# A graph layer on one core: 336 instead of 294 edge tiles picked on TensorE, their keys spread by DMA

## The chip, the cores and the metric

One core of one Trainium2 chip runs the whole kernel. The metric is device time in microseconds (us), median of the runs shown. Below, TensorE is PE in the profile, VectorE DVE, ScalarE ACT, GpSimd POOL and SyncE SP; PEld is TensorE's weight load.

## The reference

200,000 edges, sorted by destination, carry messages between 6,250 nodes of 64 features. Cut to what matters:

```python
w = silu(edge_attr_32 @ W1 + b1) @ W2 + b2                 # E x 9
h_src = x[src]                                             # a row of x for each edge
msg = einsum('ef,em,fmg->eg', h_src, edge_attr_9 * w, W_tp)
agg = segment_sum(msg, dst, 6250) / 4
emb = silu(node_vec[:, None] @ Wn1 + bn1) @ Wn2 + bn2      # gamma, beta
gamma, beta = split(emb, 2)
out = layernorm(x + agg * (1 + gamma) + beta)
```

## The kernel before

The edges form 1,563 tiles of 128, one edge to a partition, and 98 groups of 16 tiles (the last has 11). One stage `i` of the main loop works on several groups at once, as the program order has it: it gathers for group i+6, prepares i+2 and i+1, reduces i, and places i-2.

**Where `x[src]` comes from.** There are three ways, and a group uses all of them. For most tiles GpSimd issues one indirect DMA per tile (L91, `hs`), 13 a group. Every sixth group from 7 on (`SPG`, 16 groups) has its first tile loaded by SyncE row by row (L106), 128 DMAs of 256 bytes, spread over the six stages ahead with the register loads of L101. The last Q = 3 tiles of a group are *picked* by TensorE: x lies in SBUF in two fp32r parts `xs`, node number = 49 p + 7 h + l with p the partition. A tile's keys (p for each edge, and h times 128) are turned into a one-hot matrix, and 7 x 2 products of 448 columns (L482) with it fetch seven candidate rows for each edge into the PSUM tile `px`; VectorE selects the right one (L491, L493). So a picked tile costs 14 products, and an unpicked one an indirect DMA.

**How keys become one-hot matrices.** `setup` works out the keys on VectorE, turns them over on TensorE and writes them to DRAM (`kd`, L222 to L229) as bf16, the two halves in two rows. `load_keys` (L391) fetches two groups' keys onto two partitions. `keys` (L451) multiplies them with `ones2` (1 in two rows, 0 elsewhere; L458), so that every partition of the PSUM tile `pk` holds the sum of the halves for 384 edges; the fourth quarter of `pk` takes the product of `gate` (L357), and `gam` and `xb` are made from it (L358, L359). One VectorE instruction then compares the three tiles' keys with the seven node numbers of each partition (L464, `hot_k`).

**The order of the work.** The order is written by hand (`manual_schedule`), and each engine runs its instructions in that order. In stage i TensorE runs: the 14 products of pick 0 of group i+1, with `place(i-2)` (L559, `pd`) and `keys(i+2)` put between them; `hidden(i+2)` (L405); `second(i+1)` (L422); `windows(i)` (L511, `pz`), which needs all rows of group i; pick 1, with `weights(i+1)` (L432) and `project(i-1)` (L537, `pr`) between; pick 2. VectorE follows: `near` in even stages (L385), the addition of `pd` to `acc` (L563), `gam`, `xb`, `hot_k`, then L491 and L493 of pick 0, `weights` (L438, L444), `c` (L544), L491 and L493 of pick 1, in every fourth stage the ten operations of `finish_nodes`, then pick 2. ScalarE has `st` (L413), `p2s` (L425), eight copies `zt` (L521) and `r` (L542).

**Buffers.** PSUM has eight banks in use: `px` two, `pz` two, `p1` two, one under the tag "s" (`p2` of `second` and `weights`, and `pd`) and one under "r" (`pk` and `pr`). Who writes into "s" or "r" waits until the last reader of the tile before is done. `hs` has seven buffers, so GpSimd can be six groups ahead.

Of the kernel before, what the change touches and what calls it, by code (L numbers as in the profile page):

```python
# [6 lines left out]

F32 = mybir.dt.float32
I32 = mybir.dt.int32
BF16 = mybir.dt.bfloat16  # L10
F32R = mybir.dt.float32r
AF = mybir.ActivationFunctionType
ALU = mybir.AluOpType
AX = mybir.AxisListType

P = 128
N, F, M, D, H, E = 6250, 64, 9, 32, 64, 200000
NJ = 49
# [3 lines left out]
NBLK = (NT + KB - 1) // KB  # L22
# [3 lines left out]
FB = 2  # L26
AHEAD = 6
LB = 2
Q = 3
J = 7  # L30
SPG = range(7, NBLK, 6)
SPR = 22
# [16 lines left out]

def picked(g):  # L50

    return Q


def tiles(g):
# [4 lines left out]
def gnn_resnorm_kernel(ctx: ExitStack, tc: tile.TileContext, x, src, dst, dst_row, ea, sh, cn,  # L60
# [18 lines left out]
    with ExitStack() as fast:  # L79
# [35 lines left out]
        lo = keep.tile([P, NBLK], F32)  # L115
        nk = keep.tile([P, J], F32)
        li = keep.tile([P, J], F32)
        ones2 = keep.tile([P, P], BF16)
        kr2 = [keep.tile([P, LB, Q, P], BF16, name=f"kr{k}") for k in range(2)]
        zt = [keep.tile([P, 5, KB, W], F32, name=f"zt{k}") for k in range(2)]  # L120
        rel = keep.tile([P, NBLK * KB], F32)
        nid = keep.tile([P, NBLK], F32)
# [2 lines left out]
        ext = keep.tile([P, 4], F32)  # L125
        C = NBLK * Q
        jl = keep.tile([P, C], F32)
        kd = dram.tile([2, C, P], BF16, name="kd")
        cn_d = dram.tile([P, NJ], F32, name="cn_d")
        cn_v = cn_d.rearrange("p j -> (p j)")  # L130
        wn1c = keep.tile([H, 1], F32)
# [4 lines left out]
        def setup(temp):  # L136
# [52 lines left out]
            zero = temp.tile([P, 1], F32)  # L189
            nc.vector.memset(zero, 0.0)  # L190
            for k in range(2):
                nc.vector.memset(kr2[k], 0.0)
            nc.vector.memset(ones2, 0.0)
            nc.vector.memset(ones2[0:2], 1.0)
            for k in range(2):
                nc.vector.memset(zt[k][F:P, 4], 0.0)
                nc.vector.memset(ht[k][H:H + 1], 1.0)
            nc.vector.memset(wtc2[F:P, 4], 0.0)
# [20 lines left out]
            nc.vector.tensor_scalar(ti[1], rest, 37.0, None, op0=ALU.mult)  # L219
            nc.vector.tensor_scalar(ti[1], ti[1], 8, None, op0=ALU.logical_shift_right)  # L220
            nc.vector.tensor_scalar(kh, ti[1], float(P), None, op0=ALU.mult)
            for c0 in range(0, C, P):  # L222
                n = min(P, C - c0)
                p_kt = psum.tile([P, 2, P], F32, tag=("s", "r", "s")[c0 // P], name=f"p_kt{c0}")
                for i, half in enumerate((kp, kh)):
                    nc.tensor.matmul(p_kt[0:n, i, :], half[:, c0:c0 + n], ident, start=True, stop=True)
                kt = temp.tile([P, 2, P], BF16, name=f"kt{c0}")
                nc.scalar.copy(kt[0:n], p_kt[0:n])
                nc.sync.dma_start(kd[:, c0:c0 + n, :].rearrange("i c e -> c i e"), kt[0:n])  # L229
            nc.vector.scalar_tensor_tensor(jl, kh, -float(J) / P, rest, op0=ALU.mult, op1=ALU.add)  # L230
            hidden(0, act=False)
            load_keys(0)
# [33 lines left out]
            def between(h):  # L266

                if h == 0:
                    p_f = psum.tile([KB, NBLK], F32, tag="s", name="p_f")
                    nc.tensor.matmul(p_f, first_t, ident[0:NBLK, 0:NBLK], start=True, stop=True)  # L270
                    nc.scalar.copy(first_f, p_f)
                elif h == 1:
                    for f in keys(0, -1):
                        f()
                elif h == 3:
                    p_cn = psum.tile([P, NJ], F32, tag="s", name="p_cn")
                    nc.tensor.matmul(p_cn, cn_j, ident[0:NJ, 0:NJ], start=True, stop=True)
                    cn_s = temp.tile([P, NJ], F32)
                    nc.scalar.copy(cn_s, p_cn)
                    nc.sync.dma_start(cn_d, cn_s)  # L280
                    nc.sync.dma_start(wn1c, wn1.rearrange("o h -> h o"))
                    nc.sync.dma_start(bn1c, bn1.unsqueeze(1))
                    gate_load(0)
                    nc.sync.dma_start(wn2a[0:H, :], wn2)
                    nc.sync.dma_start(wn2a[H:H + 1, :], bn2.unsqueeze(0))
                    for q in range(2):
                        n = (M + 1 - q) // 2
                        nc.sync.dma_start(wtc2[q * F:(q + 1) * F, 0:n, :], wtp[:, q:M:2, :])
                    load(LB)
                    with nc.allow_non_contiguous_dma(reason="2048 words, once"):  # L290
                        nc.sync.dma_start(src_r, src[:, SPG[0] * KB:NBLK * KB:6 * KB].rearrange("p g -> g p"))
# [9 lines left out]
                    hidden_act(0)  # L301
                between(h)
            pick(0, 0)
            for f in keys(1, -1):
                f()
            base(0)
            near(0)
            second(0)
# [8 lines left out]
            ids()  # L317
            hidden(1)
            nc.scalar.copy(acc_r, zero.to_broadcast([P, NJ * F]))
            pick(0, 2)  # L320
            nc.sync.dma_start(xb, x.rearrange("(j p) f -> p j f", p=P))
            for s in range(2):
                nc.sync.dma_start(w2bd[s * H:(s + 1) * H, s, :], w2)
# [30 lines left out]
            nc.scalar.activation(ht[j0 // 4 % 2][0:H, :nj], cb.pop(j0)[:, :nj], AF.Silu, bias=bn1c, scale=wn1c)  # L354

        def gate(j, pe):
            nc.tensor.matmul(pe, ht[j // 4 % 2][:, j % 4], wn2a, start=True, stop=True)  # L357
            nc.vector.tensor_scalar(gam[:, j, :], pe[:, 0:F], 1.0, 0.25, op0=ALU.add, op1=ALU.mult)  # L358
            nc.vector.tensor_add(xb[:, j, :], xb[:, j, :], pe[:, F:2 * F])  # L359

# [29 lines left out]

        def load_keys(g):  # L391
            n = min(LB, NBLK - g)
            kr = kr2[g // LB % 2]
            nc.sync.dma_start(kr[0:2, 0:n].rearrange("i g t e -> i (g t) e"), kd[:, g * Q:(g + n) * Q, :])
            for i in range(n):
                kr_t[g + i] = kr[:, i, Q - picked(g + i):, :]

# [50 lines left out]

        hot_k = {}

        def keys(g, j):  # L451

            pk = psum.tile([P, Q + 1, P], F32, tag="r", name=f"pk{g}")
            q = picked(g)

            def part(k):
                if k == 0:
                    nc.tensor.matmul(pk[:, 0:q, :].rearrange("p t e -> p (t e)"), ones2,  # L458
                                     kr_t.pop(g).rearrange("i t e -> i (t e)"), start=True, stop=True)
                else:  # L460
                    gate(j, pk[:, Q, :])
                if k == n - 1:
                    hot_k[g] = late.tile([P, Q, J, P], F32R, tag="hot_k", name=f"hot_k{g}")
                    nc.vector.tensor_tensor(hot_k[g][:, 0:q], pk[:, 0:q].unsqueeze(2).to_broadcast([P, q, J, P]),  # L464
                                            nk[:, None, :, None].to_broadcast([P, q, J, P]), op=ALU.is_equal)

            n = 2 if 0 <= j < NJ else 1
            return [lambda k=k: part(k) for k in range(n)]

        def pick(g, t, other=()):  # L470


            other = [f for fs in other for f in fs]
            q = picked(g) if g < NBLK else 0
            if t >= q:
                for f in other:
                    f()
                return
            px = psum.tile([P, F, J], F32, tag="px", name=f"px{g}_{t}", bufs=2)
            for h in range(J):  # L480
                for i in range(2):
                    nc.tensor.matmul(px.rearrange("p f l -> p (f l)"), hot_k[g][:, t, h, :],  # L482
                                     xs[i][:, h].rearrange("p f l -> p (f l)"),
                                     start=(h == 0 and i == 0), stop=(h == J - 1 and i == 1))
                    if i == 1 and other:
                        other.pop(0)()
            for f in other:
                f()
            xm = late.tile([P, F, J], F32, tag="xm", name=f"xm{g}_{t}")
            c = (g + 1) * Q - q + t  # L490
            nc.vector.scalar_tensor_tensor(xm, li[:, None, :].to_broadcast([P, F, J]), jl[:, c:c + 1], px,  # L491
                                           op0=ALU.is_equal, op1=ALU.mult)
            nc.vector.tensor_reduce(hs[g][:, tiles(g) - q + t, :], xm, AX.X, ALU.add)  # L493
# [54 lines left out]
        def place(g):  # L548

            if not 0 <= g < NBLK:  # L550
                return []
            kb = lo_block(g)
            js = [j for j in (0, 1) if 0 <= kb + j < NJ]
            pd = {}

            def part(j):
                if j == js[0]:
                    pd[g] = psum.tile([P, 2, F], F32, tag="s", name=f"pd{g}")
                nc.tensor.matmul(pd[g][:, j, :], hot[g][:, j * P:(j + 1) * P], r[g], start=True, stop=True)  # L559
                if j == js[-1]:  # L560
                    hot.pop(g), r.pop(g)
                    b0, b1_ = kb + js[0], kb + js[-1] + 1
                    nc.vector.tensor_add(acc[:, b0:b1_, :], acc[:, b0:b1_, :], pd[g][:, js[0]:js[-1] + 1, :])  # L563

            return [lambda j=j: part(j) for j in js]

        done = 0
        with tc.manual_schedule(), tc.tile_pool(name="temp", bufs=1) as temp:
            setup(temp)

            for i in range(NBLK):
# [10 lines left out]
                for g in SPG:  # L582
                    if 0 < g - i <= AHEAD:
                        load_rows(g, (AHEAD - g + i) * SPR)
                pick(i + 1, 0, [place(i - 2)] + ([keys(i + 2, i - 2)] if i + 2 < NBLK else []))
                if 3 <= i <= 5:
                    reach(i - 3)
                if i + 2 < NBLK:
# [13 lines left out]
                while ready - done >= (FB if ready < NJ - 1 else 1):  # L602
                    finish(done, min(done + FB, ready))
                    done = min(done + FB, ready)
                pick(i + 1, 2)
                if i >= NBLK - 2:
                    windows(i)
                if i == NBLK - 2:
# [205 lines left out]
```

## Time and profile before

| | |
|---|---|
| median of 3 runs | 1590.99 us (1590.33 to 1592.33) |
| profiled execution, whole | 1590.71 us |
| its span, on which the profile's shares stand | 1588.9 us |
| TensorE clock granted, mean | 0.961 of full |
| SyncE row DMAs of 256 bytes (L106) | 2048 |
| `ea` loads (L374) | 49, of 512 KB |
| `kr` loads (L394) | 49, of 3 KB |
| DMA | 85.42 MB, mean 54 GB/s |

A group in the profile is all instructions of a line and an engine: count, busy time, mean duration in ns, then how long the engine had been idle before them and what ended that. Matmuls overlap, so that one instruction's duration is more than it adds to TensorE's time; the pitch between starts in the timeline is what counts. An fp32 matmul stands in the trace as two instructions.

### The profile page before, as it was taken

To read this page: it belongs to the slowest core of one execution; us is meant where nothing else is said; L and a number is where in the kernel's file an instruction comes from. 1 tells how busy PE (TensorE), PEld (TensorE's weight loads), DVE (VectorE), ACT (ScalarE), POOL (GpSimd) and SP (SyncE) were. 2 spreads that over 40 slices of the span, in tenths; PEclk is the share of its full clock that TensorE was granted. 3 is DMA by queue.
4 is the path that set the end of the run, shared out by engine and by line. 5 is a ranking of instruction groups with operands and counts; after the bars stand their busy time and mean duration, and the time that the engine had idled before them with its cause. 6 is when DMAs were issued, how large, how long until landed. Compare 5 with 4: busy or idle time off the path is not lost.

```text
span 1588.9 us, 33055 instructions
## 1 busy us (share of the span) xinstructions
PE 1407.5 (89%) x10206; PEld 1143.1 (72%) x10206; DVE 992.6 (62%) x1611; ACT 473.1 (30%) x1187; POOL 1186.0 (75%) x1262
## 2 busy tenths in 40 slices
PE   5999999988989888989898989888889899888886
PEld 3777778767777777777676767676777777776765
DVE  6676667665656565665665656656566666565664
ACT  4323223323232323232322323323223232322232
POOL 7777777777777777777777777777777777777773
PEclk9999999999999999999999999999999999999998
DMA  5312222221211121212111221121111211211110
GB/s 155 84 48 50 62 50 54 58 50 50 61 50 50 45 66 45 50 50 61 48 47 45 52 57 47 47 62 46 45 47 47 62 46 47 62 47 45 47 46 20
DMA packets 86199, 85.42 MB, mean 54 GB/s; under 512 B 37625, under 2 KB 52013, under 8 KB 86014
## 3 DMA queue, kind: packets, MB, share of 16 engines
q0 software_dynamic: 40096, 41.14, 11.7%
q1 hardware_dynamic: 45156, 40.44, 8.4%
q8 instruction: 83, 1.36, 0.4%
q10 hardware_dynamic: 762, 1.64, 0.3%
q14 instruction: 102, 0.84, 0.2%
HBM read 81.35 MB, written 1.78 MB: 52 GB/s over the span
## 4 chain that ended last, share of the span: by engine, by line
PE 33%; POOL 32%; issue 14%; DMA 10%; SPq 7%; DVE 2%; ACT 1%; POOLq 0%; ACTq 0%; DVEq 0%
POOL hs L91 32%; PE px L482 21%; DMA hs<-in_x_dram,src_i 9%; SPq L106 4%; PE pz L511 4%; PE pr L537 2%; PE p L405 2%; SPq L101 2%; PE p L422 1%; PE p L432 1%; PE pd L559 1%; DMA ea<-in_ea_dram 1%; DVE xm L491 0%; DVE hs L493 0%; PE pk L458 0%
## 5 line engine op out<-in xcount | busy, mean ns | idle before, releaser
L91 POOL DMA_INDIRECT hs<-in_x_dram,src_i x1253 | 1184.7, 945 | 382.6 <-issue 347.3
L482 PE MATMUL px<-xs,hot_k 128*128 128x448 f32 x4116 | 1100.4, 400 | 3.2 <-DVE xs L299 3.2
L482 PEld LDWEIGHTS px<-xs,hot_k 128*128 128x128 f32 x4116 | 717.9, 196 | 62.1 <-DVE xs L299 3.6
L491 DVE SCALAR_TENSOR_TENSOR xm<-li,jl,px 128x448 f32<-128x448 f32 x294 | 199.1, 677 | 213.0 <-PE px L482 211.2
L464 DVE TENSOR_TENSOR hot_k<-pk,nk 128x2688 fp32r<-128x2688 f32 x98 | 289.4, 2953 | 4.6 <-PE pk L458 4.6
L413 ACT ACTIVATE st<-p,b1c 128x1024 f32<-128x1024 f32 x98 | 109.1, 1114 | 560.1 <-PE p L405 559.9
L511 PE MATMUL pz<-a,hs 128*64 128x72 f32 x3126 | 135.0, 245 | 134.0 <-DMA hs<-in_x_dram,src_i 79.7
L521 ACT COPY zt<-pz 64x160 f32<-64x160 f32 (+2 forms) x784 | 213.4, 272 | 128.9 <-PE pz L511 110.8
L511 PEld LDWEIGHTS pz<-a,hs 128*64 128x64 f32 x3126 | 121.1, 151 | 177.5 <-issue 161.6
L438 DVE TENSOR_TENSOR p<-p,sh 128x72 f32<-128x72 f32 x196 | 47.3, 241 | 296.0 <-PE p L432 224.3
L537 PEld LDWEIGHTS pr<-wtc,zt 128*128 128x128 f32 x980 | 190.0, 196 | 20.8 <-ACT zt L521 5.2
L493 DVE TENSOR_REDUCE hs<-xm 128x64 f32<-128x448 f32 x294 | 182.3, 620 | 10.1
L537 PE MATMUL pr<-wtc,zt 128*128 128x64 f32 x980 | 165.0, 252 | 5.0 <-ACT zt L521 5.0
L444 DVE TENSOR_TENSOR a<-oh,p 128x1152 f32<-128x1152 f32 x98 | 132.6, 1354 | 3.3
L405 PE MATMUL p<-ea,w1bd 64*128 64x512 f32 x392 | 113.5, 657 | 5.6 <-DMA ea<-in_ea_dram 5.5
L542 ACT COPY r<-pr 128x64 f32<-128x64 f32 x98 | 20.8, 212 | 261.3 <-PE pr L537 261.3
L559 PEld LDWEIGHTS pd<-r,c 128*128 128x128 f32 x388 | 73.1, 190 | 7.3 <-ACT r L542 1.0
L422 PEld LDWEIGHTS p<-st,w2p 128*32 128x32 f32 x784 | 15.6, 109 | 74.3 <-issue 72.1
L559 PE MATMUL pd<-r,c 128*128 128x64 f32 x388 | 64.6, 249 | 0.7 <-ACT r L542 0.7
L422 PE MATMUL p<-st,w2p 128*32 128x256 f32 x784 | 63.5, 396 | 0.0
L432 PE MATMUL p<-ident,p2s 128*128 128x128 f32 x196 | 58.9, 301 | 3.9 <-ACT p2s L425 3.8
L413 ACT ACT_TABLE_LOAD x23 | 29.5, 1283 | 94.7 <-PE p L405 94.7
(103 smaller groups left out, 456.6 us busy)
## 6 DMA issues: line engine op xcount, KB each, us to landing
hs<-in_x_dram SPq DMA_DIRECT2D x2048, 0.2 KB
ea<-in_ea_dram SPq DMA_DIRECT2D x49, 512.0 KB
hs<-in_x_dram,src_i POOLq DMA_INDIRECT x1253
sh<-in_sh_dram SPq DMA_DIRECT2D x49, 144.0 KB
cb<-cn_d SPq DMA_DIRECT2D x12, 128.0 KB
out_dram<-o SPq DMA_DIRECT2D x24, 64.0 KB
gam<-in_x_dram ACTq DMA_DIRECT2D x2, 448.0 KB
dst_i<-in_dst_dram SPq DMA_DIRECT2D x1, 784.0 KB
```

Source lines behind the costliest of these rows:

```text
L91: hs_dma[g] = [nc.gpsimd.indirect_dma_start(out=hs[g][:, t - g * KB, :], out_offset=None, in_=x, in_offset=bass.IndirectOffsetOnAxis(ap=sr ...
L405: nc.tensor.matmul(p1[:, i, :], w1bd[i * 64:(i + 1) * 64, :], e[i * 64:(i + 1) * 64, :], start=True, stop=True)
L413: nc.scalar.activation(st[g], p1_t.pop(g), AF.Silu, bias=b1c)
L444: nc.vector.tensor_mul(a[g], oh_t.pop(g)[:, :, None, :].to_broadcast([P, KB, M, W]), sw.unsqueeze(3).to_broadcast([P, KB, M, W]))
L464: nc.vector.tensor_tensor(hot_k[g][:, 0:q], pk[:, 0:q].unsqueeze(2).to_broadcast([P, q, J, P]), nk[:, None, :, None].to_broadcast([P, q, J ...
L482: nc.tensor.matmul(px.rearrange("p f l -> p (f l)"), hot_k[g][:, t, h, :], xs[i][:, h].rearrange("p f l -> p (f l)"), start=(h == 0 and i ...
L491: nc.vector.scalar_tensor_tensor(xm, li[:, None, :].to_broadcast([P, F, J]), jl[:, c:c + 1], px, op0=ALU.is_equal, op1=ALU.mult)
L493: nc.vector.tensor_reduce(hs[g][:, tiles(g) - q + t, :], xm, AX.X, ALU.add)
L511: mm = nc.tensor.matmul(pz[v * F:(v + 1) * F, k // 2].rearrange("p m w -> p (m w)"), hsg[:, k0 + k, :], ag[:, k0 + k].rearrange("p m w -> ...
L521: nc.scalar.copy(z[h * F:(h + 1) * F, 0:5 - h, k0 + v:k0 + n:2, :].rearrange("p m k w -> p k m w"), pz[v * F:(v + 1) * F, 0:(n + 1 - v) // ...
L537: nc.tensor.matmul(pr[g], z[:, c].rearrange("p k w -> p (k w)"), wtc2[:, c, :], start=(c == 0), stop=(c == 4))
L559: nc.tensor.matmul(pd[g][:, j, :], hot[g][:, j * P:(j + 1) * P], r[g], start=True, stop=True)
```

## The change

1. `picked(g)` gives 4 for three groups of every seven (g mod 7 = 1, 3, 5) and 3 for the others, with Q = 4: 336 picked tiles in place of 294. The gather loop ends earlier by as many tiles. Pick 3 follows pick 2 at the end of the stage.
2. The keys are one fp16 number (p + 128 h) in place of two bf16 halves: `kd` has one row, and is made with one transpose per 128 keys. `load_keys` reads it with a partition step of zero, so that the DMA writes the same 2 KB to each of the 128 partitions (256 KB for two groups).
3. The product with `ones2` goes. ScalarE copies the keys of a group from SBUF to the PSUM tile `pk`, 384 or 512 columns; in ScalarE's order the copy stands first in the stage, after `r` and the square root of the stage before.
4. `hot_k` is made by one VectorE instruction per tile (`hots`). Two of them stand ahead of the `acc` addition in VectorE's order, the third and fourth behind L493 of pick 0. `hot_k` has seven buffers of one tile in place of two of three.
5. The gate's product stands in `place(i-2)`, ahead of its two products, and writes the second half of `pd`, in bank "s"; `gam` and `xb` follow the `acc` addition.

```diff
-Q = 3
+Q = 4
 def picked(g):
-    return Q
+    return Q - (4 * g % 7 < 4)
...
-        ones2 = keep.tile([P, P], BF16)
-        kr2 = [keep.tile([P, LB, Q, P], BF16, name=f"kr{k}") for k in range(2)]
...
-        kd = dram.tile([2, C, P], BF16, name="kd")
+        kd = dram.tile([C, P], F16, name="kd")
...
+            kf = s_f
+            nc.vector.tensor_add(kf, kp, kh)
...
-                for i, half in enumerate((kp, kh)):
-                    nc.tensor.matmul(p_kt[0:n, i, :], half[:, c0:c0 + n], ident, start=True, stop=True)
...
+                nc.tensor.transpose(p_kt[0:n], kf[:, c0:c0 + n], ident)
...
         def gate(j, pe):
-            nc.tensor.matmul(pe, ht[j // 4 % 2][:, j % 4], wn2a, start=True, stop=True)
...
         def load_keys(g):
-            kr = kr2[g // LB % 2]
-            nc.sync.dma_start(kr[0:2, 0:n].rearrange("i g t e -> i (g t) e"), kd[:, g * Q:(g + n) * Q, :])
+            kr = loads.tile([P, LB, Q, P], F16, tag="kr", name=f"kr{g}", bufs=2)
+            nc.sync.dma_start(kr[:, 0:n].rearrange("p g t e -> p (g t e)"),
+                              rows(kd[g * Q:(g + n) * Q, :].rearrange("c e -> (c e)"), P))
...
+        def keys(g):
+
+            pk_t[g] = psum.tile([P, Q, P], F32, tag="r", name=f"pk{g}")
+            nc.scalar.copy(pk_t[g][:, 0:picked(g), :], kr_t.pop(g))
+
+        def hots(g, t0, t1):
+
+            for t in range(t0, min(t1, picked(g))):
+                hot_k[g, t] = late.tile([P, J, P], F32R, tag="hot_k", name=f"hot_k{g}_{t}", bufs=7)
+                nc.vector.tensor_tensor(hot_k[g, t], pk_t[g][:, t, None, :].to_broadcast([P, J, P]),
+                                        nk.unsqueeze(2).to_broadcast([P, J, P]), op=ALU.is_equal)
...
+            pd = psum.tile([P, 4, F], F32, tag="s", name=f"pd{g}")
+            pe = pd[:, 2:4, :].rearrange("p a f -> p (a f)")
...
+                    if g < NJ:
+                        gate(g, pe)
...
+            if g < NJ:
+                parts.insert(0, lambda: nc.tensor.matmul(pe, ht[g // 4 % 2][:, g % 4], wn2a, start=True, stop=True))
...
-                pick(i + 1, 0, [place(i - 2)] + ([keys(i + 2, i - 2)] if i + 2 < NBLK else []))
+                if i + 2 < NBLK:
+                    keys(i + 2)
+                    hots(i + 2, 0, 2)
+                pick(i + 1, 0, [place(i - 2)])
+                if i + 2 < NBLK:
+                    hots(i + 2, 2, Q)
...
-                pick(i + 1, 2)
+                for t in range(2, Q):
+                    pick(i + 1, t)
```

More of the change, by code (lines that the diff above doesn't have):

```diff
@@ L9 @@
 I32 = mybir.dt.int32
-BF16 = mybir.dt.bfloat16
+F16 = mybir.dt.float16
 F32R = mybir.dt.float32r
@@ L191, in setup @@
             for k in range(2):
[L192 to L195, printed above, removed]
                 nc.vector.memset(zt[k][F:P, 4], 0.0)
@@ L221, in setup @@
             nc.vector.tensor_scalar(kh, ti[1], float(P), None, op0=ALU.mult)
+            kf = s_f
+            nc.vector.tensor_add(kf, kp, kh)
             for c0 in range(0, C, P):
                 n = min(P, C - c0)
-                p_kt = psum.tile([P, 2, P], F32, tag=("s", "r", "s")[c0 // P], name=f"p_kt{c0}")
-                for i, half in enumerate((kp, kh)):
-                    nc.tensor.matmul(p_kt[0:n, i, :], half[:, c0:c0 + n], ident, start=True, stop=True)
-                kt = temp.tile([P, 2, P], BF16, name=f"kt{c0}")
+                p_kt = psum.tile([P, P], F32, tag=("s", "r")[c0 // P % 2], name=f"p_kt{c0}")
+                nc.tensor.transpose(p_kt[0:n], kf[:, c0:c0 + n], ident)
+                kt = acc_r[:, 6 * C + c0 // 2:6 * C + c0 // 2 + P // 2].bitcast(F16)
                 nc.scalar.copy(kt[0:n], p_kt[0:n])
-                nc.sync.dma_start(kd[:, c0:c0 + n, :].rearrange("i c e -> c i e"), kt[0:n])
+                nc.sync.dma_start(kd[c0:c0 + n, :], kt[0:n])
             nc.vector.scalar_tensor_tensor(jl, kh, -float(J) / P, rest, op0=ALU.mult, op1=ALU.add)
@@ L272, in between @@
                 elif h == 1:
-                    for f in keys(0, -1):
-                        f()
+                    keys(0)
+                    hots(0, 0, Q)
                 elif h == 3:
@@ L303, in setup @@
             pick(0, 0)
-            for f in keys(1, -1):
-                f()
+            keys(1)
+            hots(1, 0, Q)
             base(0)
@@ L319, in setup @@
             nc.scalar.copy(acc_r, zero.to_broadcast([P, NJ * F]))
-            pick(0, 2)
+            for t in range(2, Q):
+                pick(0, t)
             nc.sync.dma_start(xb, x.rearrange("(j p) f -> p j f", p=P))
@@ L449, in gnn_resnorm_kernel @@
         hot_k = {}
[L451 to L468, printed above, removed]
+        pk_t = {}
+        def keys(g):
[6 more added lines that the diff above has]
+                                        nk.unsqueeze(2).to_broadcast([P, J, P]), op=ALU.is_equal)
         def pick(g, t, other=()):
@@ L481, in pick @@
                 for i in range(2):
-                    nc.tensor.matmul(px.rearrange("p f l -> p (f l)"), hot_k[g][:, t, h, :],
+                    nc.tensor.matmul(px.rearrange("p f l -> p (f l)"), hot_k[g, t][:, h, :],
                                      xs[i][:, h].rearrange("p f l -> p (f l)"),
@@ L553, in place @@
             js = [j for j in (0, 1) if 0 <= kb + j < NJ]
-            pd = {}
+            pd = psum.tile([P, 4, F], F32, tag="s", name=f"pd{g}")
+            pe = pd[:, 2:4, :].rearrange("p a f -> p (a f)")
             def part(j):
-                if j == js[0]:
-                    pd[g] = psum.tile([P, 2, F], F32, tag="s", name=f"pd{g}")
-                nc.tensor.matmul(pd[g][:, j, :], hot[g][:, j * P:(j + 1) * P], r[g], start=True, stop=True)
+                nc.tensor.matmul(pd[:, j, :], hot[g][:, j * P:(j + 1) * P], r[g], start=True, stop=True)
                 if j == js[-1]:
@@ L562, in part @@
                     b0, b1_ = kb + js[0], kb + js[-1] + 1
-                    nc.vector.tensor_add(acc[:, b0:b1_, :], acc[:, b0:b1_, :], pd[g][:, js[0]:js[-1] + 1, :])
-            return [lambda j=j: part(j) for j in js]
+                    nc.vector.tensor_add(acc[:, b0:b1_, :], acc[:, b0:b1_, :], pd[:, js[0]:js[-1] + 1, :])
+                    if g < NJ:
+                        gate(g, pe)
+            parts = [lambda j=j: part(j) for j in js]
+            if g < NJ:
+                parts.insert(0, lambda: nc.tensor.matmul(pe, ht[g // 4 % 2][:, g % 4], wn2a, start=True, stop=True))
+            return parts
         done = 0
@@ L604, in gnn_resnorm_kernel @@
                     done = min(done + FB, ready)
-                pick(i + 1, 2)
+                for t in range(2, Q):
+                    pick(i + 1, t)
                 if i >= NBLK - 2:
```

## The prediction, made before the changed kernel ran

> **What bounds the kernel now.** I read the page's busy shares first, then the chain that ended last, the costliest groups, and the timeline of TensorE.
>
> ```profile
> PE 1407.5 (89%) x10206; PEld 1143.1 (72%) x10206; DVE 992.6 (62%) x1611; ACT 473.1 (30%) x1187; POOL 1186.0 (75%) x1262
> ...
> PE 33%; POOL 32%; issue 14%; DMA 10%; SPq 7%; DVE 2%; ACT 1%; POOLq 0%; ACTq 0%; DVEq 0%
> ...
> L91 POOL DMA_INDIRECT hs<-in_x_dram,src_i x1253 | 1184.7, 945 | 382.6 <-issue 347.3
> L482 PE MATMUL px<-xs,hot_k 128*128 128x448 f32 x4116 | 1100.4, 400 | 3.2 <-DVE xs L299 3.2
> ...
> L464 DVE TENSOR_TENSOR hot_k<-pk,nk 128x2688 fp32r<-128x2688 f32 x98 | 289.4, 2953 | 4.6 <-PE pk L458 4.6
> ...
> L511 PE MATMUL pz<-a,hs 128*64 128x72 f32 x3126 | 135.0, 245 | 134.0 <-DMA hs<-in_x_dram,src_i 79.7
> ```
>
> TensorE is "89%" and GpSimd "75%", and yet GpSimd is the pace: its gathers take 945 ns each with 0.3 us of "issue" between, (1184.7 + 382.6) / 1253 = 1.251 us apiece, without a pause. 1253 of them are 1567 us of the span of 1588.9. TensorE's 134 us of idle time stand in front of `windows`, where it waits for the rows. The timeline shows both regimes:
>
> ```profile
> 75.91 0.64 PE L422 MATMUL p<-st,w2p 128*32 128x256 f32 x8
> ...
> 89.68 0.64 PE L422 MATMUL p<-st,w2p 128*32 128x256 f32 x8
> ...
> 819.79 0.64 PE L422 MATMUL p<-st,w2p 128*32 128x256 f32 x8
> 823.04 1.22 PE L511 MATMUL pz<-a,hs 128*64 128x72 f32 x32 [2.61 <-DMA hs<-in_x_dram,src_i]
> ...
> 839.38 2.19 PE L511 MATMUL pz<-a,hs 128*64 128x72 f32 x32 [2.75 <-issue]
> ```
>
> Early, while GpSimd's lead of six groups lasts, a stage takes TensorE 89.68 - 75.91 = 13.77 us (13.53 after stage 50, without the gate). From about 300 us on the stages follow 13 gathers, 16.3 us, and TensorE waits 1 to 3 us in most. So TensorE has room, and GpSimd lacks it.
>
> **The gain on GpSimd.** 42 gathers fewer. Group 95's `windows` starts at 1545.91 and waits for nothing, within 1 us of its last gather's landing: there the two engines meet. Up to that group 329 tiles will be picked in place of 288, so its rows are there 41 x 1.251 = 51.3 us sooner, at 1494.6. What follows is TensorE's, ScalarE's and VectorE's own work to the end, 1588.9 - 1545.9 = 43.0, and a fourth pick of group 96. A pick: sixteen products at 811.96 reach to 815.35, 0.2094 each, so 14 are 2.93. The span by GpSimd: 1494.6 + 43.0 + 2.9 = 1540.5.
>
> **The same moment by TensorE.** In a stage the product with `ones2` goes; starts in the timeline move by 0.18 for it (its 337 ns overlap the next). The gate's product only changes its place. Group 95's `windows` by TensorE:
> group 0's at 50.96; 49 stages with gate of 13.77 - 0.18, 665.9; 46 without of 13.53 - 0.18, 614.1; 41 fourth picks, 120.1; 24 times 0.85, since in the stage after a `finish` ScalarE's table load (1283 ns) makes `p2s` late (the gap at 154.59); once 5.4 for `reach`, at 120 us. Sum 1476.9. That is 17.7 us ahead of GpSimd, only 0.19 us per stage. A fourth pick makes a stage 16.5 us where GpSimd needs 15.0, but the next, 13.6 against 16.3, makes it good. So the question is what new waits TensorE gets.
>
> *Keys by DMA and ScalarE.* A `kr` load rises from 3 KB to 256 KB. The first `kr` of before lands 1.3 us after its issue, 512 KB of `ea` 3.48 after; 256 KB taken half way, 2.4 (between 1.3 and 3.5). It is issued almost a stage ahead of its use, so in the loop it is hidden; if SyncE came 7 us later than now, `hots` would wait. SyncE's issue grows from 0.26 to about 0.45, 0.1 per stage on its 14.1 us (rows issued at 150.97, 164.92, 179.25, 193.18), less than the new mean stage of 15.4: behind it queue `ea` and the row DMAs. The 12.8 MB more go beside 53 GB/s at a DMA share of 0.2: gathers keep their pitch even in the first 50 us, where the share is 0.61; I take 0. ScalarE's copy of 512 columns: by the `zt` copies (160 in 286 ns, 128 in 259) 0.6 us, by the strided L297 (448 in 916) 1.04; I take 0.6, as the keys are contiguous. Either way it runs after `r`, some 3 us before the stage begins, ahead of nothing urgent: ScalarE waits there for `hidden` (559.9 us of idle). In `setup` it isn't hidden: the copy stands in ScalarE's row of `xs` copies and waits for the larger load, about 2 us, and four comparisons for group 1 take 1.1 us more than one for three. Head +3 (0 to 6).
>
> *Comparisons in single tiles, gate in bank "s".* `second` writes "s" and has to wait for `xb`, which now stands behind two `hots`. [...] TensorE asks for "s" after 2.93 + 0.22 (gate) + 0.34 (`pd`) + 1.06 (L405) = 4.55. [...] `ea` loads that come late cost some 7 us before, at stages of 13.77; longer stages ease that, 5 stays.
>
> So 1476.9 + 3 + 7 + 3 + 5 = 1494.9 by TensorE, 1494.6 by GpSimd: the two are even. Then neither repays the other's bad stages, and I add 2.5 for that: span 1540.5 + 0.3 + 2.5 = 1543.3. The profiled execution took 1590.71, 1.8 more than its span and 0.3 less than the median. Forecast 1545.
>
> [...]
>
> **The rivals.**
> *GpSimd stays the pace throughout* (part of my forecast's case): the new waits come to less than 10 us: 1540.5 + 1.8 = 1542. For it: the margin above. Against: it is thin.
> [...]
> *Slower than before:* bank "s" handed from VectorE to TensorE in each stage. If `hots` start only when a late `kr` or a ScalarE stuck in `finish` lets `pk` be written, `second`, `windows` and all that follow move. It takes (1591 - 1545) / 95 = 0.5 us per stage over the forecast to be even; 0.7 gives 1611. Against: the copy has about 3 us of lead and `kr` a stage.
> *The gathers don't get cheaper in number as they do in time:* if 256 KB bursts slow the pitch from 1.251 to 1.28, 1211 of them take 35 us more, 1580. Nothing in the busy first 50 us speaks for it.
>
> **How the numbers follow.** Even or GpSimd at the pace, 1541 to 1549: 0.57. TensorE at the pace, 1549 to 1575: 0.30. Slower pitch: 0.04. No change to be told: 0.02. Slower: 0.07. A measurement tells 0.2% (3 us) from no change. Range 1540 to 1567: all of the first case and most of the second. Faster 0.91, same 0.02, slower 0.07.
>
> **What would show it.** L91 1211 times at a pitch of 1.25; L482 4704 products, 0.2094 apart; no L458; ScalarE's key copy near 0.5 to 0.6 us; each comparison near 1.09, VectorE up by about 75 + 55 us; idle time before `windows` down from 134 to under 30; 16.3 to 16.6 us for a stage with four picks. New waits of `second` on `xb` and of `pr` on `hots`, of more than 15 us in all, would put TensorE at the pace. A changed gather pitch, or idle time before `windows` that stays above 60 us, would make the working wrong.

## The result, and the profile after

The changed kernel takes 1543.09 us (median of 4 runs, 1542.02 to 1543.80), the kernel before 1591.62 us beside it (4 runs). The ratio is 0.9695, 95% interval 0.9679 to 0.9712. The forecast was 1545, range 1540 to 1567. The profiled execution took 1542.02 us, its span is 1540.0 and its mean granted TensorE clock 0.984 (before 0.961).

From the page of the changed kernel: the busy shares, the chain that ended last, and the groups that answer to those shown of before.

```profile
PE 1457.7 (95%) x10688; PEld 1220.4 (79%) x10688; DVE 1094.4 (71%) x1930; ACT 519.4 (34%) x1286; POOL 1146.9 (74%) x1220
...
PE 59%; POOL 18%; DMA 8%; issue 8%; DVE 4%; SPq 2%; ACT 1%; POOLq 0%; DVEq 0%; ACTq 0%
...
L91 POOL DMA_INDIRECT hs<-in_x_dram,src_i x1211 | 1145.6, 946 | 369.8 <-issue 336.0
L474 PE MATMUL px<-xs,hot_k 128*128 128x448 f32 x4704 | 1169.3, 385 | 8.6 <-DVE xs L294 8.0
...
L459 DVE TENSOR_TENSOR hot_k<-pk,nk 128x896 fp32r<-128x896 f32 x336 | 351.5, 1081 | 2.5 <-ACT pk L453 2.5
...
L503 PE MATMUL pz<-a,hs 128*64 128x72 f32 x3126 | 122.4, 232 | 32.1 <-DMA hs<-in_x_dram,src_i 17.6
```

The gathers are 42 fewer and as dear as before: (1145.6 + 369.8) / 1211 = 1.251 us. TensorE is busy in 95% of the span, and its part of the last chain has gone from 33 to 59%, GpSimd's from 32 to 18%. The idle time before `windows` is 32 us, where it was 134. This looks as if TensorE had become the pace. Its row of the wait list and its timeline say when it is:

```profile
PE pz L503 <- DMA hs<-in_x_dram,src_i: 17.6, 12, 2.9
...
PE pz L503 <- issue: 12.0, 9, 2.4
...
PE p L419 <- DVE xb L355: 3.2, 6, 0.6
PE p L419 <- DVE acc L554: 3.1, 8, 0.4
```

```profile
342.60 0.64 PE L419 MATMUL p<-st,w2p 128*32 128x256 f32 x8
...
356.08 0.64 PE L419 MATMUL p<-st,w2p 128*32 128x256 f32 x8
...
369.57 0.64 PE L419 MATMUL p<-st,w2p 128*32 128x256 f32 x8
...
385.86 0.64 PE L419 MATMUL p<-st,w2p 128*32 128x256 f32 x8
...
399.92 0.64 PE L419 MATMUL p<-st,w2p 128*32 128x256 f32 x8 [0.50 <-DVE xb L355]
...
1495.22 1.22 PE L503 MATMUL pz<-a,hs 128*64 128x72 f32 x32 [1.22 <-DMA hs<-in_x_dram,src_i]
```

In the wait list the columns are the total in us, how many times, and the longest. In the timeline the step from one `second` (L419) to the next is a stage: 13.48 and 13.49 us with three picks, 16.29 with four, 14.06 after a `finish`. Between about 165 and 873 us TensorE never waits for gathered rows: there it spends the lead of six groups that GpSimd has at the start. From 873 us on it waits in places, 32 us in all (the lines of L503), and group 95's `windows`, where prediction and kernel can be compared, still stands waiting for its last gather, at 1495.22 (forecast 1494.6). So GpSimd holds the end, and TensorE has time in hand.

### The profile page after: what moved, and what is told of

It is laid out like the page before. It is cut to its first block, busy times and chain, and to the rows that moved or that the text cites. A ratio compares the mean times of both kernels' runs of the same rounds, so it can differ in the third digit from the quotient of the medians.

```text
span 1540.0 us, 34002 instructions
## 1 busy us (share of the span) xinstructions
PE 1457.7 (95%) x10688; PEld 1220.4 (79%) x10688; DVE 1094.4 (71%) x1930; ACT 519.4 (34%) x1286; POOL 1146.9 (74%) x1220
## 2 busy tenths in 40 slices
DMA packets 91545, 96.76 MB, mean 63 GB/s; under 512 B 37465, under 2 KB 51755, under 8 KB 91356
## 4 chain that ended last, share of the span: by engine, by line
PE 59%; POOL 18%; DMA 8%; issue 8%; DVE 4%; SPq 2%; ACT 1%; POOLq 0%; DVEq 0%; ACTq 0%
PE px L474 41%; POOL hs L91 18%; DMA hs<-in_x_dram,src_i 6%; PE pz L503 5%; PE p L402 4%; PE pr L529 4%; PE p L419 2%; PE pd L550 1%; PE p L429 1%; SPq L106 1%; DMA ea<-in_ea_dram 1%; DVE xm L483 1%; PE pd L560 1%; DVE hs L485 0%; SPq L101 0%
## 5 line engine op out<-in xcount | busy, mean ns | idle before, releaser
L91 POOL DMA_INDIRECT hs<-in_x_dram,src_i x1211 | 1145.6, 946 | 369.8 <-issue 336.0
L474 PE MATMUL px<-xs,hot_k 128*128 128x448 f32 x4704 | 1169.3, 385 | 8.6 <-DVE xs L294 8.0
L474 PEld LDWEIGHTS px<-xs,hot_k 128*128 128x128 f32 x4704 | 815.4, 191 | 68.5 <-DVE xs L294 8.8
L483 DVE SCALAR_TENSOR_TENSOR xm<-li,jl,px 128x448 f32<-128x448 f32 x336 | 228.0, 679 | 251.9 <-PE px L474 251.7
L459 DVE TENSOR_TENSOR hot_k<-pk,nk 128x896 fp32r<-128x896 f32 x336 | 351.5, 1081 | 2.5 <-ACT pk L453 2.5
L485 DVE TENSOR_REDUCE hs<-xm 128x64 f32<-128x448 f32 x336 | 208.3, 620 | 11.6
L503 PEld LDWEIGHTS pz<-a,hs 128*64 128x64 f32 x3126 | 108.2, 139 | 73.5 <-issue 66.8
L503 PE MATMUL pz<-a,hs 128*64 128x72 f32 x3126 | 122.4, 232 | 32.1 <-DMA hs<-in_x_dram,src_i 17.6
L435 DVE TENSOR_TENSOR p<-p,sh 128x72 f32<-128x72 f32 x196 | 47.3, 242 | 132.6 <-PE p L429 66.8
L419 PEld LDWEIGHTS p<-st,w2p 128*32 128x32 f32 x784 | 15.7, 108 | 82.0 <-issue 34.4
L419 PE MATMUL p<-st,w2p 128*32 128x256 f32 x784 | 63.5, 396 | 6.3 <-DVE xb L355 3.2
L402 PEld LDWEIGHTS p<-ea,w1bd 64*128 64x128 f32 x392 | 30.1, 188 | 30.8 <-issue 25.8
L429 PE MATMUL p<-ident,p2s 128*128 128x128 f32 x196 | 54.3, 278 | 0.0
```

The costliest lines, as they stand in the source:

```text
L91: hs_dma[g] = [nc.gpsimd.indirect_dma_start(out=hs[g][:, t - g * KB, :], out_offset=None, in_=x, in_offset=bass.IndirectOffsetOnAxis(ap=sr ...
L402: nc.tensor.matmul(p1[:, i, :], w1bd[i * 64:(i + 1) * 64, :], e[i * 64:(i + 1) * 64, :], start=True, stop=True)
L419: nc.tensor.matmul(p2[g][c * D:(c + 1) * D, 0, :].rearrange("p (i e) -> p i e", i=2), w2p, s[:, :, c * P:(c + 1) * P], start=True, stop=True)
L459: nc.vector.tensor_tensor(hot_k[g, t], pk_t[g][:, t, None, :].to_broadcast([P, J, P]), nk.unsqueeze(2).to_broadcast([P, J, P]), op=ALU.is_ ...
L474: nc.tensor.matmul(px.rearrange("p f l -> p (f l)"), hot_k[g, t][:, h, :], xs[i][:, h].rearrange("p f l -> p (f l)"), start=(h == 0 and i ...
L503: mm = nc.tensor.matmul(pz[v * F:(v + 1) * F, k // 2].rearrange("p m w -> p (m w)"), hsg[:, k0 + k, :], ag[:, k0 + k].rearrange("p m w -> ...
```

## The experiments

Times are medians; the kernel before was run beside each. Experiments 1 to 4 ran on one chip, where the kernel before takes 1591.69 us (1590.15 to 1592.65).

**1. The keys by the product again** (336 picks, everything else of the change kept; `kr` is loaded to one partition of a tile that is zero elsewhere).

```diff
...
-            nc.scalar.copy(pk_t[g][:, 0:picked(g), :], kr_t.pop(g))
+            nc.tensor.matmul(pk_t[g][:, 0:picked(g), :].rearrange("p t e -> p (t e)"), ones2,
+                             kr_t.pop(g).rearrange("p t e -> p (t e)"), start=True, stop=True)
```

> The changed kernel with one thing put back: each stage's keys go to PSUM by a product with a row of ones on TensorE (fp16, one row), at the place where ScalarE's copy stood, and the key load writes one partition. Theory: GpSimd's gathers set the end, TensorE has only 33 us in hand (its waits for rows in the changed kernel). The product costs TensorE about 0.28 us a stage, 26 us, and ScalarE's table load waits for TensorE again, 24 x 0.85 = 20 us, so the 33 us are used up and some 13 us over: 1552 to 1560. Rival, only the number of gathers counts and the way of the keys is free: 1543.

Measured: 1541.49 us (1540.98 to 1542.77), ratio 0.9689 (0.9675 to 0.9704): as fast as the changed kernel. My number was missed. The wait list, the timeline of TensorE and the groups of ScalarE by form, all of this kernel:

```profile
PE pz L510 <- DMA hs<-in_x_dram,src_i: 7.5, 4, 2.6
...
PE p L435 <- ACT p2s L428: 6.4, 13, 0.6
```

```profile
308.34 0.39 PE L459 MATMUL pk<-kr,ones 128*128 128x512 f16 x1
308.38 0.75 PE L481 MATMUL px<-xs,hot_k 128*128 128x448 f32 x2
```

```profile
L416 ACT ACT_TABLE_LOAD x23 | 29.5, 1283 | 117.5 <-PE p L408 117.5
```

The product lasts 0.39 us, but the next starts beside it; a three-pick stage is 13.67 us where the changed kernel has 13.49, and one with four 16.52 where it has 16.28. Over 96 stages that is some 20 us, and the waits behind ScalarE's table load (L435 in the first fence, L416 in the third) bring some 11 more with their gaps; the head is 3.6 us shorter (`kr` is small again; that this is the reason is not shown). Net that is about 27 us of TensorE's time. It doesn't reach the end: TensorE's waits for gathered rows (the lines of L510) fall from 32 to 12 us in all, and group 95's `windows` starts at 1494.40, behind its gather. So the theory's mechanism holds (GpSimd is the pace and TensorE's slack swallows the product), and its sizes don't: I had put the product at 0.28 per stage and the slack at 33.

**2. Three picks everywhere** (294 picks, everything else of the change kept).

```diff
-    return Q - (4 * g % 7 < 4)
+    return Q - 1
```

> The changed kernel with three picks in every group (294), everything else of the change kept. Theory: 1253 gathers at 1.251 us set the end as before, so 1588 to 1593, and TensorE's idle time ahead of windows rises well over before's 134 us, to about 180, because it lost the product and the late table loads. Rival, keys by DMA and ScalarE bring part of the gain by themselves: 1545 to 1575.

Measured: 1591.71 us (1590.86 to 1592.61), ratio 1.0001 (0.9992 to 1.0011), as the theory had it; the rival (1545 to 1575) falls. From its page and its wait list:

```profile
L91 POOL DMA_INDIRECT hs<-in_x_dram,src_i x1253 | 1186.3, 947 | 382.6 <-issue 349.4
...
L503 PE MATMUL pz<-a,hs 128*64 128x72 f32 x3126 | 141.7, 252 | 129.0 <-DMA hs<-in_x_dram,src_i 84.6
```

```profile
PE pz L503 <- DMA hs<-in_x_dram,src_i: 84.6, 45, 3.4
PE pz L503 <- issue: 34.2, 17, 3.1
PE p L402 <- DMA ea<-in_ea_dram: 15.8, 15, 2.6
```

The gathers are again 1253, and the time is that of before to 0.01%. Keys by DMA, the copy on ScalarE, single comparisons and the gate in bank "s" together bring nothing by themselves. What they free on TensorE is not seen as more idle time before `windows` (129 us; I had expected about 180). Part of it went into other waits: 15.8 us for `ea`, where the kernel before has 5.5, and 10.6 at `second` (L419 in that list), where it has none. Another part went into slow restarts (experiment 4): of stages 6 to 95, taken from one `windows` to the next, the granted clock falls below 0.97 in 31, against 25 in the kernel before; its mean is 0.949, against 0.961. How the rest divides is not worked out.

**3. Four picks in every other group** (343 picks).

```diff
-    return Q - (4 * g % 7 < 4)
+    return Q - (g % 2 == 0)
```

> The changed kernel with four picks in every odd group and three in every even one: 343 picks. Theory: 7 gathers less are 8.8 us less on GpSimd, 7 picks of 2.80 us are 19.6 of TensorE's 33 us in hand, so GpSimd still sets the end: 1533 to 1537. Rival, TensorE is already the pace over the whole run, as the prediction's sum had it (no time in hand): 1543 + 20 = 1563.

Measured: 1535.37 us (1535.15 to 1535.49), ratio 0.9648 (0.9635 to 0.9661). Seven gathers fewer should save 7 x 1.251 = 8.8 us by GpSimd's pace; 7.7 came. The rival (TensorE even with GpSimd, 1563) falls. This is the best of the versions tried, 3.5% under the kernel before and 0.5% under the changed one. TensorE's waits for gathered rows are down to the 10.3 and 6.2 us of these lines:

```profile
PE pz L503 <- DMA hs<-in_x_dram,src_i: 10.3, 7, 2.1
...
PE pz L503 <- issue: 6.2, 6, 2.0
```

**4. Four picks in four groups of seven** (350 picks).

```diff
-    return Q - (4 * g % 7 < 4)
+    return Q - (4 * g % 7 < 3)
```

> The changed kernel with four picks in four groups of seven: 350 picks. Theory: GpSimd would end 17.5 us sooner, but TensorE needs 14 x 2.80 = 39 us and has 33 in hand, so TensorE sets the end: 1546 to 1551, slower than with 343 picks. Rival, GpSimd's count alone: 1526.

Measured: 1538.60 us (1537.42 to 1539.46), ratio 0.9670 (0.9656 to 0.9685). That is neither: GpSimd alone would have given 1526, and I had forecast 1546 to 1551. Its page and its wait list:

```profile
PE 1484.7 (97%) x10884; PEld 1248.3 (81%) x10884; DVE 1126.4 (73%) x1972; ACT 517.9 (34%) x1286; POOL 1135.1 (74%) x1206
...
PE 79%; POOL 5%; DVE 4%; DMA 4%; issue 3%; SPq 3%; ACT 1%; DVEq 0%; POOLq 0%; ACTq 0%
```

```profile
PE pz L503 <- DMA hs<-in_x_dram,src_i: 0.7, 3, 0.3
```

TensorE is the pace here: it waits 0.7 us for gathered rows in the whole run. That makes this run a measure of what TensorE needs. Group 95's `windows` starts at 1487.96, with 13 more picks behind it than in the changed kernel. A pick adds 16.28 - 13.49 = 2.8 us to a stage, so in the changed kernel TensorE alone would, by this estimate, be there at 1487.96 - 13 x 2.8 = 1451.6. It was there at 1495.2: 43.6 us in hand, not the 32 of its waits. About half of the difference shows in the timelines. First the changed kernel, then this one, one stage with four picks each:

```profile
919.21 0.64 PE L419 MATMUL p<-st,w2p 128*32 128x256 f32 x8
921.90 1.37 PE L503 MATMUL pz<-a,hs 128*64 128x72 f32 x32 [2.06 <-DMA hs<-in_x_dram,src_i]
...
938.92 0.64 PE L419 MATMUL p<-st,w2p 128*32 128x256 f32 x8
```

```profile
963.92 0.64 PE L419 MATMUL p<-st,w2p 128*32 128x256 f32 x8
964.49 1.22 PE L503 MATMUL pz<-a,hs 128*64 128x72 f32 x32
...
979.98 0.64 PE L419 MATMUL p<-st,w2p 128*32 128x256 f32 x8
```

The stage without a wait takes 16.06, the one with a wait of 2.06 takes 19.71, which is 1.6 more than wait and stage together; its `windows` takes 1.37 in place of 1.22. Two stretches of the changed kernel show the cause, and that it does not follow every wait. The first is the stage from 921.90 on, the second one of four picks behind a longer wait; the third number from the end is the granted clock:

```profile
999.25 1.22 PE L503 MATMUL pz<-a,hs 128*64 128x72 f32 x32 [2.37 <-issue]
...
921.90:939.40 17.50, 17.50 (x116) 14.87 (x116) 11.53 (x24) 6.11 (x14) 13.23 (x15) 0.90 0.23 47
999.25:1015.30 16.05, 16.05 (x116) 13.68 (x116) 9.40 (x16) 3.43 (x11) 12.17 (x13) 1.00 0.29 70
```

After the wait of 2.06 the clock is 0.90 over the stage and 1.5 us are lost; after the wait of 2.37 it is full and nothing is lost. The changed kernel has eleven waits of 1.6 us or more before `windows`. Four (1.93, 2.06, 2.55 and 2.88) are followed by a stage at 0.90, seven (1.61 to 2.42) are not, so the length alone doesn't decide, and what does is open. These four restarts cost some 6 of the 11.6 us between 32 and 43.6; the rest is spread over the head and single stages. Some of what a long wait costs is thus not in the wait list, and it comes back when the wait goes.

**5 to 9. Runs that settle nothing.** The remaining runs fell on three other chips, on which the kernel before itself takes 2386 to 2388 us at a granted clock of 0.80 to 0.82, so none of their numbers can be set against those above.

*Gathers apart from TensorE's work* (42 more gathers, into a tile that nobody reads, with 336 picks; in `gather`):

```diff
+            if picked(g) == Q:
+                spare = gath.tile([P, F], F32, tag="spare", name=f"spare{g}", bufs=2)
+                t = g * KB + tiles(g) - 1
+                nc.gpsimd.indirect_dma_start(
+                    out=spare, out_offset=None, in_=x,
+                    in_offset=bass.IndirectOffsetOnAxis(ap=src_i[:, t:t + 1], axis=0))
```

> The changed kernel with one more indirect DMA in each group of four picks: 42 gathers into a tile that nothing reads, so that GpSimd issues 1253 again while TensorE does 336 picks. Theory: the time goes back to that of before, 1590 to 1596 (41 gathers of 1.251 us up to group 95 are 51 us). Rival, the gain came from TensorE and the way of the keys: 1543.

Measured: 2617.06 us, 1.0949 (1.0919 to 1.0979) of the kernel before on that chip.

*All comparisons ahead of the `acc` addition:*

```diff
-                    hots(i + 2, 0, 2)
+                    hots(i + 2, 0, Q)
...
-                    hots(i + 2, 2, Q)
```

> The changed kernel with all three or four comparisons of a group ahead of the acc addition in VectorE's order, in place of two ahead and the rest behind pick 0. Theory: bank s is handed over just in time, so each comparison moved ahead (1.01 us) is a wait of TensorE at second, about 1.0 us a stage and 94 in all; less the 43 us that the run with 350 picks showed TensorE to have in hand: 1580 to 1605. Rival, VectorE's order is hidden: 1543.

Measured: 2640.13 us, 1.1063 (1.1043 to 1.1084).

*Keys loaded once* (`load_keys` gives the first tile for all later groups; it leaves out the later loads, so later groups pick the wrong rows):

```diff
+            if g > LB:
+                for i in range(n):
+                    kr_t[g + i] = kr_1[0][:, i, Q - picked(g + i):, :]
+                return
...
```

> The changed kernel without the key loads after the first two: 47 DMAs of 256 KB left out, so all later groups use the keys of the first two and their picked rows are not those asked for. Theory: the loads are hidden and gathers keep their pitch of 1.251 us, so 1541 to 1544. Rival, 12 MB more of DMA slow the gathers or make the ea loads late: 3 to 10 us faster than the changed kernel, 1533 to 1540.

Measured: 2571.90 us, 1.0770 (1.0744 to 1.0796). These three had also been run on another such chip, with the same outcome to 0.3% (2622.39, 2641.44 and 2571.23).

*The product again, with 350 picks* (edits 1 and 4 together), where TensorE is the pace and the product can't hide; run on two such chips:

> 350 picks, where TensorE sets the end (1538.6 with the keys by DMA and ScalarE), with the keys by the product again. Theory: here the product and the late table loads have no cover. By the run with 336 picks they cost 0.18 to 0.24 us a stage, 20 us, and 11 for the table loads, less 3 for an earlier start: 1562 to 1570. Rival, the way of the keys is free here too: 1536 to 1541.

> 350 picks (three, four, three, four ... by 4g mod 7 below 3 take three) with the keys to PSUM by the product of the first experiment instead of ScalarE's copy. Theory: with 350 picks TensorE sets the pace (its waits for picked rows were 0.7 us in the run of 350 picks), so here the product is paid in full: 98 stages by the 0.2 us that it cost per stage in the first run and some 10 us of waits at the second from the table load, 1538.6 + 27 = 1566 us (1560 to 1572). Rival (the product costs nothing that matters, as in the first run, so ScalarE's copy brings nothing): 1536 to 1544 us.

Measured: 2590.92 us, 1.0867 (1.0841 to 1.0893), and 2582.18, 1.0798 (1.0769 to 1.0827). From the page of the first of the five (42 more gathers):

```profile
L91 POOL DMA_INDIRECT hs<-in_x_dram,src_i x1211 | 1147.1, 947 | 1302.3 <-PE pz L509 945.7
...
L489 DVE SCALAR_TENSOR_TENSOR xm<-li,jl,px 128x448 f32<-128x448 f32 x336 | 227.9, 678 | 1214.1 <-remote 947.8
```

Here GpSimd waits 945.7 us for `windows` to give `hs` back, so TensorE's side is the pace and GpSimd isn't; and VectorE waits 947.8 us for a releaser that the trace can't name. On such a chip all of these kernels with 336 or 350 picks are 8 to 11% slower than the one with 294. It would fit that a pick costs where TensorE is the pace and saves where GpSimd is, but the changed kernel itself didn't run there, nor is there a profile of the kernel before from there, and the cause of the pauses is open. Whether the order of the comparisons, the key loads or the product matter with 350 picks on an undisturbed chip stays open too.

## Why the prediction was right

The forecast's case was "even or GpSimd at the pace". What happened is the half of it that stands as the first rival: GpSimd throughout (1542), with far more room on TensorE than I gave it. GpSimd's side of the sum carries the number. TensorE's side was 43 us too high, and that it landed within 0.3 us of GpSimd's, and so did not spoil the forecast, was luck.

**GpSimd's side held.** 42 gathers fewer at an unchanged pitch: 1.251 us forecast, 1.251 measured, with 96.76 MB moved in place of 85.42. Group 95 at 1494.6 forecast, 1495.2 measured; from there to the end 45.9 forecast, 44.8 measured. Experiments 2 and 3 confirm that the picks alone carry the gain: with 42 fewer picks it is all gone, with 7 more it grows by 7.7 us.

**TensorE's side did not.** I had it at 1494.9, "the two are even"; by experiment 4 it is at about 1451.6, so my sum was 43 us too high. The 2.8 us that I added for being even (0.3 and 2.5) were not needed, and make up most of the 3.3 by which the forecast span of 1543.3 exceeds the 1540.0 measured. The mis-sized terms, forecast first:

| term of TensorE's sum | forecast | measured |
|---|---|---|
| wait behind ScalarE's table load | 24 x 0.85 = 20.4 | 0 |
| three-pick stage, with gate | 13.59 | 13.49 |
| fourth pick | 2.93 | 2.79 |
| head, up to group 0's `windows` | 50.96 + 3 = 54.0 | 55.6 |
| `reach`, in its stage and the next | +5.4 | +6.6 |
| first two stages, shorter than the others | 0 | -2.1 |
| `second` on `xb` or `acc` | 7 | 7.3 with its gaps |
| first `pr` on `hots` | 3 | 0 |
| waits for `ea` | 5 | 1.5 |

In us saved against the forecast: 20.4 + 95 x 0.10 + 41 x 0.14 - 1.6 - 1.2 + 2.1 - 0.3 + 3 + 3.5 = 41.1 of the 43.3. The remaining 2 I can't place.

*The largest term, the table load, is a fact of the program that I did not look up.* Before, ScalarE's timeline has the load waiting, and `st` behind it:

```profile
147.23 0.30 ACT L635 ACTIVATE var<-var,eps 128x2 f32<-128x2 f32 x1 [1.66 <-DVE var L634]
151.76 1.28 ACT L413 ACT_TABLE_LOAD   x1 [4.23 <-PE p L405]
153.06 1.11 ACT L413 ACTIVATE st<-p,b1c 128x1024 f32<-128x1024 f32 x1
```

In the changed kernel it doesn't wait, and 1.28 us disappear in ScalarE's idle time:

```profile
158.31 0.30 ACT L637 ACTIVATE var<-var,eps 128x2 f32<-128x2 f32 x1 [1.71 <-DVE var L636]
158.51 0.47 ACT L453 CAST pk<-kr 128x384 f32<-128x384 f16 x1
159.00 1.28 ACT L410 ACT_TABLE_LOAD   x1
162.52 1.11 ACT L410 ACTIVATE st<-p,b1c 128x1024 f32<-128x1024 f32 x1 [2.24 <-PE p L402]
```

The program as built shows the reason. `st` needs two semaphores, one of TensorE and one of ScalarE's own. Before, it carries only one of them; the other has an instruction of its own, and the table load stands behind that:

```
before   L413 EventSemaphore [waits PE]          L413 LoadActFuncSet   L413 Activation st [waits Activation]
after    L453 TensorCopy pk [waits Activation]   L410 LoadActFuncSet   L410 Activation st [waits PE]
```

The key copy has already waited for ScalarE's own semaphore, so `st` needs only TensorE's, and the load is free to run ahead. The traces count the separate waits in `st`'s line, before, after, and in experiment 1, which takes the copy away again:

```profile
L413 ACTq EVENT_SEMAPHORE  x97: 17/17/17, 15.8 to 1545.5; - x97
...
L410 ACTq EVENT_SEMAPHORE  x1: 17/17/17, 16.4 to 16.4; - x1
...
L416 ACTq EVENT_SEMAPHORE  x97: 17/17/17, 16.3 to 1492.5; - x97
```

In experiment 1 the wait of the load is back with them (117.5 us in front of it in its line, and the 6.4 us of L435). So the copy does bring TensorE something that I had not counted, besides the product.

*Slow restarts.* I counted 16 of them in the kernel before and gave them nothing in the sum: in 16 stages `windows` takes 2.0 to 2.2 us in place of 1.22 (at 839.38, behind a wait of 2.75, it takes 2.19, and the granted clock is 0.90 up to the next `windows`). The granted clock falls below 0.97 in 25 of the stages 6 to 95 of the kernel before, and in 4 of the changed kernel's, while the idle time before `windows` fell from 134 to 32 us: with fewer gaps came fewer slow restarts. What they cost is seen only where TensorE's own time is measured (experiment 4).

*The pick's pitch.* I wrote 0.2094 for sixteen products from 811.96 to 815.35. These two starts give 3.39 / 16 = 0.212, and they take in the step from the last product to `pd`, which I spread over the products. The stage measures 0.200 (2.79 / 14).

**What I had doubted and what held.** Key copies of 0.48 and 0.59 us (0.6 forecast), well ahead of their use: `hot_k` waits 2.5 us for them in all. Two comparisons on end:

```profile
366.38 2.08 DVE L459 TENSOR_TENSOR hot_k<-pk,nk 128x896 fp32r<-128x896 f32 x2
368.37 0.28 DVE L554 TENSOR_TENSOR acc<-acc,pd 128x128 f32<-128x128 f32 x1
...
368.70 0.21 DVE L355 TENSOR_TENSOR xb<-xb,pd 128x64 f32<-128x64 f32 x1
```

Two take 1.99 us from start to start, 1081 ns being the mean duration of one, and `xb` is done at 368.91, 0.66 us before `second` asks at 369.57. In even stages `near` takes some 0.4 of that (0.42 each). So the single comparisons cost TensorE nothing in such a stage. After a `finish` the wait is there, 0.57 (14.06 against 13.49). The slower rival, bank "s" handed over in each stage, didn't come: waits of L419 are 6.3 us in all. VectorE's busy time grew by 102 us (forecast 130). No run of the kernel before shows what a single comparison takes, nor the two terms of TensorE's sum that rest on it, 7 for `second` and 3 for the first `pr`: they were my estimates, and the changed kernel showed 7.3 and 0.

## What to carry to other kernels

When one engine sets the pace and another waits for it, work moved from the first to the second pays almost one for one until the second has no wait left, and changes that only relieve the waiting engine pay nothing by themselves: 42 gathers off GpSimd (52.5 us) brought 48.5, all the other changes alone 0.0. To find how far this goes, do not take the slack from the wait list (32 us here) but push past the crossing point once (experiment 4: 43 us), and take the best amount between (343 picks, of the three amounts tried). And before charging a wait to an instruction, look which instruction of the built program carries the semaphore: an unrelated one in front of it can take the wait over.

## What the runs showed of the hardware that was not expected

- One wait of an activation can stand on an instruction of its own in front of the table load, so that the 1.283 us of the load are not hidden (94.7 us of idle time in front of 23 loads before, 0.4 after).
- Some waits of TensorE of about 2 to 3 us cost 1.5 to 1.6 us more behind them, at a granted clock of 0.90 over the stage: 4 of 11 in the changed kernel. A wait of 2.42 did not, one of 1.93 did.
- Gathers keep their pitch of 1.251 us with the DMA traffic up by 13% and 256 KB loads beside them.
- On three chips the kernel before took 2386 to 2388 us in place of 1591, at a clock of 0.80 to 0.82.
